# First attention: what keys to the left add, put into the strips ahead of their way through DRAM

## The chip, the cores and the metric

The kernel runs on one core of a Trainium2 chip. Its engines work side by side, each through its own queue in order: TensorE (PE: matrix products and transposes, results in PSUM), VectorE (DVE), ScalarE (ACT), GpSimd (POOL) and SyncE (SP), which here only issues DMA transfers. Engines wait for each other and for transfers by semaphores. The metric is the device time of one execution in microseconds, lower being better; for the kernel before it is 2069.74 us, the median of three runs (2066.32 to 2071.68).

## The reference, cut to what matters

The program is a stack of four layers, each added to its input: an attention with relative positions, a feed-forward layer, a second attention and a mixture of experts. Only the first attention is touched. It has 8 batches of 512 tokens, 16 heads of 16 numbers:

```python
pos_k = (rel_embeddings @ Wk + bk)             # 128 positions, per head
c2p_att = einsum('bhqd,hpd->bhqp', q, pos_k)   # query by position
c2p = take_along_axis(c2p_att, clip(rel + 64, 0, 127), axis=-1)
p2c_att = einsum('bhkd,hpd->bhkp', k, pos_k)   # key by position
p2c = swapaxes(take_along_axis(p2c_att, clip(-rel + 64, 0, 127), -1), -1, -2)
scores = (q @ k.T + c2p + p2c) / scale         # scale = sqrt(48)
probs = softmax(scores); ctx = probs @ v
```

`rel` is a bucket of the distance query minus key. Distances of 127 and more, to the left or to the right, all give the first or the last position. So a score gets two terms that depend on the distance, and each is constant far away on either side.

## The kernel before, in words

The first attention (`_l0_attention`) goes through 256 steps, numbered in the order of `steps`: batch b (8), group g of four heads (4), tile i of 128 queries (4), pair p of two heads (2). Eight steps are thus one head group, and i runs from 0 to 3 in it, two steps each.

*Strips.* For each step `strips(u)` multiplies 128 queries by 256 position columns, and 128 keys by 256 columns, for two heads (eight matmuls, L364). Column c of a strip belongs to one distance (127 - c for queries, c - 127 for keys), up to column 254. Distances beyond are the same on each side; the kernel measures the near values from the end values, so that far keys add nothing here, and folds the end values into the products of query and key through spare rows. What is then missing is a constant for keys on the left within the query's own block of 128 keys (and the like on the key side). That constant comes out of the same matmul as column 255 of the strip.

Two ACT copies bring a strip from PSUM to SBUF (L371). SP writes it to one of four DRAM buffers (`shift`, L381, 255 columns of 512). Reading it back with rows of 511 instead of 512 shifts each row by its number: distances turn into places, and the near blocks come out as query by key. Two reads do that (L390): `winp` holds the key side, which still has to be transposed, and `winc` the query side.

*The own block.* POOL multiplies column 255 by a mask of the keys on the left (`own`, L374; the masks are `later` and `earlier`, triangles of 128 by 128 in `aside`). When the reads have landed, `add()` puts `own` on the middle block of `winp` and on the block i of `winc` (two POOL adds of 128x256, L401).

*A step.* The products of query and key go into PSUM (L421). `near_keys` transposes blocks of `winp` on top of them (L433): its own block, the left and the right neighbour's. The right neighbour of step n is step n+2, which has the next i; for i = 3 there is none. DVE adds `winc` and takes the row minimum of the negated scores (L447), ACT makes the exponentials (L450), TensorE turns them (L461), DVE copies them (L464) and TensorE multiplies them by the values (L473).

*Order.* The order on every engine is written by hand (`tc.manual_schedule`). In step n come the first product, `strips(n + 5)`, then `near_keys(n)`, the rest of the products' work and what `plan` holds for that step (projections of the next group, L174; the output and layer norm of an earlier batch, L509 to L523, with POOL adds). Inside `strips(u)` the order of the issues is: own(u) on POOL, the write of u on SP, the two reads of u-1 on SP, the adds of u-2 on POOL. The reads of u-1 therefore stand behind the write of u in SP's queue.

*Buffers.* Strips have three SBUF buffers, own three, winp eight, winc eight; DRAM buffers are four.

Of the kernel before, what the change touches and what calls it, by code (L numbers as in the profile page):

```python
# [12 lines left out]
F32 = mybir.dt.float32  # L13
# [3 lines left out]
ALU = mybir.AluOpType  # L17
# [4 lines left out]
P = 128  # L22
# [6 lines left out]
W = 256  # L29
# [61 lines left out]
def _l0_attention(nc, tc, a, x, ident, mhalf, carry, prefetch):  # L91
# [6 lines left out]
    with ExitStack() as ctx:  # L98
# [20 lines left out]
        def load(b):  # L119
            nc.sync.dma_start(x[b], a["x"][b].rearrange("(t p) c -> p t c", p=P))  # L120
# [7 lines left out]
        def busy(n, w):  # L128

            idle = misc("idle")  # L130
            for _ in range(n):
                nc.tensor.matmul(idle, w[:, :P], w[:, :S], start=True, stop=True)
# [57 lines left out]
        with tc.tile_pool(name="a_pos", bufs=1) as pp:  # L190
# [14 lines left out]
            nc.sync.dma_start(rows["bv"], a["bv"].partition_broadcast(P))  # L205

            aside = wp.tile([P, 2, P], F32, tag="aside", name="aside")
            nc.sync.dma_start(aside[:, 0, :], a["later"])
            nc.sync.dma_start(aside[:, 1, :], a["earlier"])
            zeros = pp.tile([P, 8 * W], F32, tag="zeros", name="zeros")  # L210
            nc.gpsimd.memset(zeros, 0.0)
            for d in shift:
# [116 lines left out]
        sb = pool("a_sb", 2)  # L329
# [4 lines left out]
        def near(i):  # L334

            lo, hi = max(0, i - 1), min(NT, i + 2)
            return lo, hi, (lo - i + 1) * P, (hi - i + 1) * P
# [1 line left out]

        steps = [(b, g, i, p) for b in range(B) for g in range(NG) for i in range(NT) for p in range(2)]  # L340
        wins, totals = {}, {}
        reads, adds = [], []
        cns = {b: [] for b in range(B)}
        rest = []
        def project(b, g):
# [6 lines left out]
        def heads(p):  # L352

            return [slice(32 * r, 32 * r + 32) for r in (2 * p, 2 * p + 1)]

        def strips(u, between=None):


            b, g, i, p = steps[u]
            s = sm[b, g]  # L360
            pas = [ps_a.tile([P, S], F32, tag="psa", name="pa") for j in range(2)]
            for t, (src, pos) in enumerate(((s[0], posc), (s[2], posp))):
                for pa, rs in zip(pas, heads(p)):
                    nc.tensor.matmul(  # L364
                        pa[:, t * W : (t + 1) * W], src[rs, i * P : (i + 1) * P], pos[rs, g, :], start=True, stop=True
                    )
                if t == 0 and between is not None:
                    between()
            st = sb.tile([P, 4, W], F32, tag="strip", name="strip", bufs=3)
            for j in range(2):  # L370
                nc.scalar.copy(st[:, 2 * j : 2 * j + 2, :].rearrange("p t w -> p (t w)"), pas[j])  # L371

            own = sb.tile([P, 2, 2, P], F32, tag="own", name="own", bufs=3)
            nc.gpsimd.tensor_tensor(  # L374
                own,
                aside.unsqueeze(2).to_broadcast([P, 2, 2, P]),
                st[:, :, W - 1 : W].rearrange("p (j t) o -> p t j o", t=2).to_broadcast([P, 2, 2, P]),
                ALU.mult,
            )
            d = shift[u % NSHIFT]  # L380
            nc.sync.dma_start(  # L381
                bass.AP(d.tensor, d.offset + P + 1, [[2 * W, P], [2 * W * P, 4], [1, W - 1]]), st[:, :, : W - 1]
            )
            wc = winc[u % (2 * NT)]
            wk_ = sb.tile([P, 2, WIN], F32, tag="winp", name="winp", bufs=8)

            def read():
                lo, hi, c0, c1 = near(i)
                for t, dst in ((1, wk_[:, :, c0:c1]), (0, wc[:, :, lo * P : hi * P])):
                    nc.sync.dma_start(  # L390
                        dst,
                        bass.AP(
                            d.tensor,
                            d.offset + t * 2 * W * P + P + c0,
                            [[2 * W - 1, P], [4 * W * P, 2], [1, c1 - c0]],
                        ),
                    )

            def add():
                for t, dst in ((1, wk_[:, :, P : 2 * P]), (0, wc[:, :, i * P : (i + 1) * P])):  # L400
                    nc.gpsimd.tensor_tensor(dst, dst, own[:, t], ALU.add)  # L401


            reads.append(read)
            adds.append(add)
            if len(reads) > 1:
                reads.pop(0)()
            if len(adds) > 2:
                adds.pop(0)()
            wins[u] = wc, wk_  # L410

        def products(n):
# [142 lines left out]
        with tc.manual_schedule():  # L555
            for f in first:
                f(1)
            for u in range(AHEAD):
                strips(u)
                if u >= 2:  # L560
                    load(3 + u)
                if u < AHEAD - 1:
                    busy(1, posc[:, 0:2].rearrange("p g w -> p (g w)"))
            es, ets = None, deque()
            for now in range(len(steps) + 3):
                n = now
                if n < len(steps):
                    b, g, i, p = steps[n]
                    if (i, p) == (0, 0):
                        if g % 2 == 0:  # L570
                            totals[b, g // 2] = sb.tile([P, NT, 8], F32, tag="totals", name="totals", bufs=2)
                    scs, parts = products(n)
                    parts.pop(0)()
                    more = parts.pop() if parts else None
                    if n + AHEAD < len(steps):
                        strips(n + AHEAD, more)
                    else:
                        if more is not None:
                            more()
                        for todo in (reads, adds):  # L580
                            if todo:
                                todo.pop(0)()
                    new = []
                    for j in range(2):
                        near_keys(n, j, scs[j])
                        new.append(weights(n, j, scs[j]))
                if n <= len(steps):
                    if es:
                        ets.extend(turned(es))
                    es = new  # L590
                if n % 2 and len(ets) >= 4:
                    four = [ets.popleft() for _ in range(4)]
                    weigh(n - 3, four, 0)
                elif n % 2 == 0 and n >= 4:
                    weigh(n - 4, four, 1)
                for f in plan.pop(n, ()):
                    f()
                for f in prefetch.get(n - len(steps), ()):
                    f(misc, sb)
            for n in sorted(plan):  # L600
                for f in plan[n]:
                    f()
# [1075 lines left out]
def _buckets(r):  # L1678

    d = np.abs(r)  # L1680
    d = np.where(d < 32, 31, d)
    far = np.ceil(np.log(d / 32) / np.log(127 / 32) * 31 - 1e-6) + 32
    return np.where(d <= 32, d, far * np.sign(r)).astype(np.int64)


def _constants():
    onehot = np.zeros((2, P, W), np.float32)
    j = np.arange(W - 1)
    for t, r in enumerate((127 - j, j - 127)):
        place = 64 - _buckets(-r) if t else 64 + _buckets(r)  # L1690
        onehot[t, np.clip(place, 0, 127), j] += 1.0
        onehot[t, np.where(r > 0, 127, 0), j] -= 1.0
    m = np.arange(P)
    tail = np.zeros((P, 2), np.float32)
    for e, t, value in ((HD, 0, 1.0), (HD + 1, 0, -1.0), (HD + 2, 1, -SCALE), (HD + 3, 1, SCALE)):
        tail[m % 32 == e, t] = value
    i = np.arange(4)
    heads = np.zeros((P, NK, 32), np.float32)
    for k in range(NK):
        heads[m, k, NH // NK * k + m // HD] = 1.0  # L1700

    tiles = np.arange(NB).reshape(B // 2, 2, 2, 2).transpose(2, 0, 1, 3).reshape(NB)
    before = (i[None, :] < i[:, None]).astype(np.float32).reshape(16)
    return {
        "onehot": onehot,
        "tail": tail,
        "later": np.tril(np.ones((P, P), np.float32), -1),
        "before": before,
        "heads": heads,
        "pages": (P * (m[:, None] + P * np.arange(2))).astype(np.float32),  # L1710
        "earlier": np.triu(np.ones((P, P), np.float32), 1),
        "dest": (
            (P * tiles[None, :, None] + m[:, None, None]) * TOPK + np.arange(TOPK)
        ).astype(np.int32),
        "spare": (NTOK * TOPK + P * np.arange(NS)[None, :] + m[:, None]).astype(np.int32),
    }
# [20 lines left out]
def _layout(v):  # L1737
# [26 lines left out]
        "supT": v["L1_ffn_shared_up_w"].T,  # L1764
        "sdownT": v["L1_ffn_shared_down_w"].T,
        **_constants(),
    }

# [16 lines left out]
```

## Time and profile before

| what | value |
|---|---|
| median of three runs | 2069.74 us |
| the profiled execution | 2061.48 us |
| its span, first to last instruction | 2059.7 us |
| TensorE busy | 1937.6 us (94%) |
| DVE busy | 1392.4 us (68%) |
| ACT busy | 1106.3 us (54%) |
| POOL busy | 1134.0 us (55%) |
| DMA traffic | 444.46 MB, mean 216 GB/s |
| write of a strip, issue to landing | 510 KB, 4.3 us (median) |
| read of winp, issue to landing | 384 KB 4.9 us, 256 KB 4.3 us |
| read of winc, issue to landing | 384 KB 6.3 us, 256 KB 4.4 us |

In the profile a group of instructions is named by its line, engine, operation and tiles (written tile, arrow, read tiles), followed by its count, its busy time, the mean of one in ns, and how long the engine stood idle just before such an instruction and what ended most of that. PEld is TensorE's loading of weights, SPq the issuing of a DMA by SP. The first attention takes the span up to about 1070 us.

### The profile page before, as it was taken

To read this page: it belongs to the slowest core of one execution; us is meant where nothing else is said; L and a number is where in the kernel's file an instruction comes from. 1 tells how busy PE (TensorE), PEld (TensorE's weight loads), DVE (VectorE), ACT (ScalarE), POOL (GpSimd) and SP (SyncE) were. 2 spreads that over 40 slices of the span, in tenths; PEclk is the share of its full clock that TensorE was granted. 3 is DMA by queue.
4 is the path that set the end of the run, shared out by engine and by line. 5 is a ranking of instruction groups with operands and counts; after the bars stand their busy time and mean duration, and the time that the engine had idled before them with its cause. 6 is when DMAs were issued, how large, how long until landed. Compare 5 with 4: busy or idle time off the path is not lost. (4 is left out here: it accounts for less than half of the span.)

```text
span 2059.7 us, 49676 instructions
## 1 busy us (share of the span) xinstructions
PE 1937.6 (94%) x18040; PEld 1327.0 (64%) x18040; DVE 1392.4 (68%) x3727; ACT 1106.3 (54%) x2368; POOL 1134.0 (55%) x1334
## 2 busy tenths in 40 slices
PE   7999999999999999999989999999989877899997
PEld 4666666676666766766656666655555444588886
DVE  4677777677777777766776555247876786456666
ACT  3776777767777777776742211344444333144443
POOL 4666777867778677776744111014434443455555
PEclk9999999999999999999999999999999997999999
DMA  9999999999999999999974446801111114557888
GB/s 296 317 317 281 296 300 295 300 285 307 295 298 303 289 310 303 294 298 289 294 224 141 124 127 195 25 0 37 43 38 45 48 45 190 208 164 219 258 262 272
DMA packets 387522, 444.46 MB, mean 216 GB/s; under 512 B 43472, under 2 KB 368080, under 8 KB 386768
## 3 DMA queue, kind: packets, MB, share of 16 engines
q1 hardware_dynamic: 372496, 401.94, 64.3%
q0 software_dynamic: 13824, 38.29, 5.1%
q8 instruction: 146, 2.39, 0.5%
q10 hardware_dynamic: 960, 1.05, 0.2%
q14 instruction: 96, 0.79, 0.1%
HBM read 238.99 MB, written 202.19 MB: 214 GB/s over the span
## 5 line engine op out<-in xcount | busy, mean ns | idle before, releaser
L447 DVE CUSTOM_DVE_ANT_0 e<-sc,winc 128x512 f32<-128x512 f32 x512 | 333.3, 689 | 289.9 <-PE sc L433 174.1
L450 ACT ACTIVATE e<-e,low 128x512 f32<-128x512 f32 x512 | 365.6, 715 | 101.8 <-DVE low L447 100.3
L371 ACT COPY strip<-pa 128x512 f32<-128x512 f32 x512 | 275.2, 591 | 129.1 <-POOL winc L401 53.1
L374 POOL TENSOR_TENSOR own<-aside,strip 128x512 f32<-128x512 f32 x256 | 268.8, 1050 | 113.4 <-ACT strip L371 97.6
L464 DVE COPY et<-et_ps 128x512 f32<-128x512 f32 x512 | 328.5, 683 | 0.7 <-PE et_ps L461 0.7
L421 PE MATMUL sc<-sm,sm 32*128 32x256 f32 (+3 forms) x1792 | 310.0, 436 | 0.7 <-DVE low L447 0.4
L364 PE MATMUL pa<-pos,sm 32*128 32x256 f32 x2048 | 292.1, 401 | 0.1
L941 POOL DMA_INDIRECT rows<-pay,slot x128 | 141.1, 1103 | 220.3 <-issue 207.1
L401 POOL TENSOR_TENSOR winp<-winp,own 128x256 f32<-128x256 f32 x256 | 187.2, 731 | 106.3 <-DMA winp<-shift 83.7
L433 PE MATMUL sc<-ident,winp 128*128 128x128 f32 x1280 | 203.7, 287 | 30.0 <-DMA winp<-shift 29.5
L421 PEld LDWEIGHTS sc<-sm,sm 32*128 32x128 f32 x1792 | 164.3, 185 | 96.8 <-DVE et L464 35.2
L401 POOL TENSOR_TENSOR winc<-winc,own 128x256 f32<-128x256 f32 x256 | 187.1, 731 | 68.3 <-DMA winc<-shift 61.4
L941 POOL DMA_INDIRECT results<-y,r x160 | 156.3, 977 | 119.6 <-ACT y L1560 77.4
L433 PEld LDWEIGHTS sc<-ident,winp 128*128 128x128 f32 x1280 | 137.6, 142 | 108.1 <-issue 57.2
L461 PE MATMUL et_ps<-ident,e 64*128 64x64 f32 x4096 | 184.2, 230 | 1.1 <-DVE et L464 1.1
L364 PEld LDWEIGHTS pa<-pos,sm 32*128 32x128 f32 x2048 | 176.1, 185 | 10.8 <-ACT strip L371 3.9
L58 POOL TENSOR_TENSOR rstd<-var,mhalf 128x2 f32<-128x2 f32 (+1 forms) x56 | 51.0, 911 | 233.8 <-DVE var L56 210.1
L461 PEld LDWEIGHTS et_ps<-ident,e 64*128 64x128 f32 x4096 | 148.8, 140 | 44.1 <-issue 22.1
L473 PE MATMUL ctx_ps<-et,v 128*32 128x128 f32 x4096 | 168.2, 283 | 0.5 <-DVE et L464 0.5
L1540 PE MATMUL pge<-store,rT 128*128 x640 | 166.1, 382 | 1.8 <-DMA r<-rows 0.8
L174 PE MATMUL pq<-xnT,wqk 128*128 128x512 f32 x256 | 132.8, 643 | 0.7 <-PE pv L156 0.7
L738 ACT ACTIVATE hT<-ph,b 128x512 f32<-128x512 f32 x64 | 44.0, 687 | 165.6 <-PE ph L735 165.6
(222 smaller groups left out, 3340.0 us busy)
## 6 DMA issues: line engine op xcount, KB each, us to landing
shift<-strip SPq DMA_DIRECT2D x256, 510.0 KB, 4.3
winp<-shift SPq DMA_DIRECT2D x128, 384.0 KB, 4.9
winc<-shift SPq DMA_DIRECT2D x128, 384.0 KB, 6.3
winp<-shift SPq DMA_DIRECT2D x128, 256.0 KB, 4.3
winc<-shift SPq DMA_DIRECT2D x128, 256.0 KB, 4.4
rows<-empty SPq DMA_DIRECT2D x8, 2640.0 KB, 13.6
r<-rows SPq DMA_DIRECT2D x160, 132.0 KB, 2.7
z<-results SPq DMA_DIRECT2D x32, 512.0 KB, 5.6
```

The source lines that it names most:

```text
L364: nc.tensor.matmul(pa[:, t * W : (t + 1) * W], src[rs, i * P : (i + 1) * P], pos[rs, g, :], start=True, stop=True)
L371: nc.scalar.copy(st[:, 2 * j : 2 * j + 2, :].rearrange("p t w -> p (t w)"), pas[j])
L374: nc.gpsimd.tensor_tensor(own, aside.unsqueeze(2).to_broadcast([P, 2, 2, P]), st[:, :, W - 1 : W].rearrange("p (j t) o -> p t j o", t=2).t ...
L401: nc.gpsimd.tensor_tensor(dst, dst, own[:, t], ALU.add)
L421: nc.tensor.matmul(sc[:, c0:c1], s[side_][rs, cut : cut + P], s[2 + side_][rs, c0:c1], start=c0 == 0, stop=False, skip_group_check=True,)
L433: nc.tensor.matmul(sc[:, m * P : (m + 1) * P], wins[n + 2 * (m - i)][1][:, j, (i - m + 1) * P : (i - m + 2) * P], ident, start=False, stop ...
L447: nc.vector.tensor_tensor_reduce(e, sc, wins[n][0][:, j, :], 1.0, -LOW, ALU.add, ALU.min, low)
L450: nc.scalar.activation(e, e, AF.Exp, bias=low, scale=-1.0, accum_out=totals[b, g // 2][:, i, r : r + 1])
L461: nc.tensor.transpose(bank[:, c : c + 64], e[rs, m * P : (m + 1) * P], ident[rs, rs])
L464: nc.vector.tensor_copy(et[:, f].rearrange("p j m q -> p (j m q)"), bank)
L473: nc.tensor.matmul(ctx_ps[32 * r : 32 * r + 32, i * P : (i + 1) * P], vs[b % 2][:, m, g % 2, g // 2 * 4 + r, :], et[:, :, m, :], start=m = ...
L941: ins = nc.gpsimd.indirect_dma_start(to, bass.IndirectOffsetOnAxis(ap=index, axis=0), source, None, bounds_check=last)
```

## The change

The constant is added to the strip in SBUF, before it is written to DRAM, instead of to `winp` and `winc` after they were read. In a strip the own block isn't a block: row m of a strip has its left keys of the own block where m + c is at least 127 and c is under 127 (query side), or, on the key side, where the column past 128 and m sum to under 127. One array `aside` with these two masks takes the place of the two triangles. `own` is laid out as the strip is (head, side), and one POOL add of 128x512 elements puts it on the first half of the query side's columns and on the second half of the key side's, for both heads. The list `adds` and its function go.

```diff
             aside = wp.tile([P, 2, P], F32, tag="aside", name="aside")
-            nc.sync.dma_start(aside[:, 0, :], a["later"])
-            nc.sync.dma_start(aside[:, 1, :], a["earlier"])
+            nc.sync.dma_start(aside, a["aside"])
...
-            own = sb.tile([P, 2, 2, P], F32, tag="own", name="own", bufs=3)
+            own = sb.tile([P, 2, 2, P], F32, tag="own", name="own", bufs=2)
             nc.gpsimd.tensor_tensor(
                 own,
-                aside.unsqueeze(2).to_broadcast([P, 2, 2, P]),
-                st[:, :, W - 1 : W].rearrange("p (j t) o -> p t j o", t=2).to_broadcast([P, 2, 2, P]),
+                aside.unsqueeze(1).to_broadcast([P, 2, 2, P]),
+                st[:, :, W - 1 : W].rearrange("p (j t) o -> p j t o", t=2).to_broadcast([P, 2, 2, P]),
                 ALU.mult,
             )
+            nearer = st.rearrange("p (j t) (h r) -> p j (t h) r", t=2, h=2)[:, :, 0:4:3, :]
+            nc.gpsimd.tensor_tensor(nearer, nearer, own, ALU.add)
             d = shift[u % NSHIFT]
             nc.sync.dma_start(
                 bass.AP(d.tensor, d.offset + P + 1, [[2 * W, P], [2 * W * P, 4], [1, W - 1]]), st[:, :, : W - 1]
...
-            def add():
-                for t, dst in ((1, wk_[:, :, P : 2 * P]), (0, wc[:, :, i * P : (i + 1) * P])):
-                    nc.gpsimd.tensor_tensor(dst, dst, own[:, t], ALU.add)
             reads.append(read)
-            adds.append(add)
             if len(reads) > 1:
                 reads.pop(0)()
-            if len(adds) > 2:
-                adds.pop(0)()
...
-                        for todo in (reads, adds):
-                            if todo:
-                                todo.pop(0)()
+                        if reads:
+                            reads.pop(0)()
...
-        "later": np.tril(np.ones((P, P), np.float32), -1),
+        "aside": np.stack([(m + m[:, None] >= 127) * (m < 127), m + m[:, None] < 127], 1).astype(np.float32),
```

More of the change, by code (lines that the diff above doesn't have):

```diff
@@ L341, in _l0_attention @@
         wins, totals = {}, {}
-        reads, adds = [], []
+        reads = []
         cns = {b: [] for b in range(B)}
```

## The prediction

> **What bounds the kernel now.** I read the page's 40 slices first. The change touches the first attention alone, which is the first half of the span, and there TensorE is full while the DMA engines look full too. These are the rows of TensorE, of its granted clock and of the DMA engines, a digit being a tenth of full:
>
> ```profile
> PE 7999999999999999999989999999989877899997
> ...
> PEclk9999999999999999999999999999999997999999
> DMA  9999999999999999999974446801111114557888
> ```
>
> Two full rows can't both be the bound, so I asked for busy time by stretch. From 60 to 1060 us, the steady part of the first attention, TensorE works 975.5 of 1000 us:
>
> ```profile
> 60.00:1060.00 1000.00, 975.50 (x13580) 678.01 (x13582) 727.31 (x1823) 725.59 (x1640) 723.83 (x907) 0.99 0.95 298
> ```
>
> The columns are PE, PEld, DVE, ACT, POOL, then clock, DMA share, GB/s. TensorE sets the pace; the other engines have a quarter of their time free. The waits of TensorE in that stretch say what takes the rest:
>
> ```profile
> PE sc L433 <- DMA winp<-shift: 23.9, 18, 4.5
> PE sc L433 <- POOL winp L401: 0.4, 1, 0.4
> ```
>
> Nearly all its idle time is the near-key transposes (L433) waiting for a strip to come back from DRAM (total us, times, longest). So TensorE is just ahead of a long chain: strip matmuls (L364), two ACT copies (L371), a DMA write to DRAM (L381), a DMA read back (L390), then L433 of a later step. The timeline shows one strip (number 114) go through it:
>
> ```profile
> 486.52 1.07 ACT L371 COPY strip<-pa 128x512 f32<-128x512 f32 x2 [0.33 <-issue]
> ...
> 487.62 0.36 SPq L381 DMA_DIRECT2D shift<-strip  x1
> 487.74 1.05 POOL L374 TENSOR_TENSOR own<-aside,strip 128x512 f32<-128x512 f32 x1
> ...
> 492.89 0.36 SPq L390 DMA_DIRECT2D winp<-shift  x1
> ...
> 495.84 0.33 PE L433 MATMUL sc<-ident,winp 128*128 128x128 f32 x1
> ...
> 497.19 0.55 PE L433 MATMUL sc<-ident,winp 128*128 128x128 f32 x3 [1.02 <-DMA winp<-shift]
> ```
>
> The copy ends at 487.59 and the write goes out at once; POOL's own (L374) runs beside the write and delays nothing. The read is issued 5.3 us later, and TensorE, having done one transpose of step 112, stands 1.02 us until it lands.
>
> How much room there is follows from the code: strip u is made in step u-5, and step u-2 already needs its winp (right neighbour), except where i is 3. That is three steps. From the starts and landings in the trace (steps 16 to 247, means): matmuls' end to copies' end 1.18 us, issue 0.05, write 4.65, wait for the read's issue 0.36, read 4.65: 10.9 us, against three steps of 3.99 = 12.0. Subtracting each landing from the moment TensorE needs it gives a mean room of 1.4 us over 174 such steps; 151 have under 2.5 us, 24 have none. By place: at i=0, first pair, 0.4; at i=2, first pair, 1.26; others 1.2 to 2.3.
>
> **The change part by part.** On POOL it removes two adds of 128x256 per strip and puts in one of 128x512. The rows (busy us, mean ns, idle before):
>
> ```profile
> L374 POOL TENSOR_TENSOR own<-aside,strip 128x512 f32<-128x512 f32 x256 | 268.8, 1050 | 113.4 <-ACT strip L371 97.6 <-DMA x<-in_x 7.3
> L401 POOL TENSOR_TENSOR winp<-winp,own 128x256 f32<-128x256 f32 x256 | 187.2, 731 | 106.3 <-DMA winp<-shift 83.7 <-PE sc L433 8.4 <-PE pa L364 8.0
> L401 POOL TENSOR_TENSOR winc<-winc,own 128x256 f32<-128x256 f32 x256 | 187.1, 731 | 68.3 <-DMA winc<-shift 61.4 <-DVE low L447 4.1 <-ACT e L450 1.4
> ...
> L1120 POOL TENSOR_TENSOR x<-x,bproj 128x512 f32<-128x512 f32 x16 | 19.9, 1271 | 0.2
> ```
>
> The new add isn't in this trace. Nearest is L1120, two full operands of that size: 1.27 us. Bounds: 1.05 (L374, one operand a broadcast) and 1.46 (two L401). I take 1.27. POOL saves 256 x (1.46 - 1.27) = 49 us of work, worth nothing: it is 72% busy. Its waits for reads go; who waited for its adds were TensorE (4.6 us) and DVE (8): I credit 4 us.
>
> *The added wait.* The write now waits for own and the add, so per strip: 0.14 (copy to own's start, in the timeline 487.59 to 487.74) + 1.05 + 1.27 + about 0.06 to issue = 2.5 us later. The amount of DMA is the same. Behind the write on SP stands the read of the strip before it, so that goes later by the same 2.5 us; for that read TensorE waits. Nothing is taken off the path in exchange: the removed adds stood behind the read, but step u-2 uses blocks of winp that they don't touch, and the own block has some 8 us of room.
>
> *What of 2.5 us reaches TensorE.* A stall lets the strips already on their way catch up; strips made after it are late again. Those are needed from three steps on. Of eight steps (one head group), the two at i=3 need no new strip. So a group has two stalls: at i=0 (room 0.4, so 2.1 us) and, three or four steps later, at i=2 (room 1.26, so about 1.3; it covers what i=1 lacks). 32 groups x 3.4 = 109 us. Low end: if phases even out, only the loop of eight bounds. The read of strip u is issued behind the write of u+1, so from those matmuls 1.2 + 2.5 + 0.45 + 4.65 = 8.8 us must fit two steps; three such links and two free steps of 3.3 make 33.0 us against 8 x 3.99 = 31.9 now: 1.1 x 32 = 36 us. High end: 2.5 twice per group, 160.
>
> *POOL's queue.* In seven batches the layer norm's adds (L521 to L523, six of 0.73 us in each of two steps) stand before own. Today own is late by 2.6 us there (strip copied at 632.66, own at 635.22) and hurts nobody; now the write is late too. About 4 us a batch: +27 (0 to 60).
>
> *Clock.* Around a 1.9 us wait at 623 us the granted clock (the third number from the end) falls:
>
> ```profile
> 623.00:626.00 3.00, 1.14 (x18) 0.78 (x20) 0.37 (x1) 1.07 (x2) 0.72 (x1) 1.00 0.96 296
> 626.00:630.00 4.00, 4.00 (x28) 1.88 (x24) 2.79 (x8) 1.52 (x4) 2.56 (x4) 0.57 1.05 362
> ```
>
> After each of five waits of 2.0 to 3.2 us in this stage the next strips came 1.2 to 1.6 us late; after three of 0.9 to 1.2 us they did not. The Trainium skill (TensorE: Matmul & The Clock Gate, "Why this matters for your kernels") asks only that gaps stay under about 3 us. By the rule, stalls of about 2 us cost nothing more; by the row, some 16 new ones over 2 us (half of the 32 at i=0) cost 1.5 each: +24 (the sum below is 104 by the rule, 128 by the row). I take the row.
>
> *Transfers.* A stalled TensorE leaves the DMA engines emptier. The skill (DMA: Bandwidth & Descriptors, "Anatomy of one DMA") fits 2.0 us plus bytes / 436 GB/s on POOL's path: 3.2 us for the 510 KB write and 2.8 for an average 320 KB read, 6.0 together. That speaks against a loss: 3.3 us shorter than 9.3 would swallow the 2.5, and the sum would be nothing or a little below. The trace's shortest are 3.4 and 3.2, the means 4.65 each. Most of this lies in the write and two reads running side by side, which stays. Groups of eight steps with a slower mean step (3.6 to 4.3 us) show no shorter writes (correlation -0.01) and hardly shorter reads (-0.17), so by the row I take 5% off: 0.47 us at each of 64 stalls, -30 (0 to -90 at 15%).
>
> *Small things.* The first step's fill: +2.5. One load for aside instead of two, and two own buffers for three (add and next own are on one engine, in order): 0.
>
> Sum: 109 + 27 + 24 - 30 - 4 + 2.5 = 128. The profiled execution took 2061.5 us (span 2059.7), so 2190; the median of the runs shown, 2069.74, lies 8 above it. With 130 I forecast **2200 us** as median.
>
> **The rivals.**
> *A: phases even out.* Stalls shrink to the loop's own bound, +36: 2106. For it: 24 steps only have no room now. Against it: projection steps (4.8 us) and plain ones (3.1 to 3.2) alternate, and room can't be carried over them.
> *B: POOL's queue and the clock bite fully.* 160 + 60 + 32 x 1.5 - 30 = 238: 2308; halfway there, about 2255, is likelier. For it: waits and dips come together in the trace. Against it: most groups show only one place with under 1 us of room.
> *C, the other side: landings shorten.* If write and read together fell from 9.3 to 6.8 us, the 2.5 would be hidden and even today's 24 us of waits partly go: 2050 to 2070. It decides from 6.8 us down; the shortest seen are 3.4 + 3.2 = 6.6, so every transfer would have to run at its best. The DMA row at 9 speaks for it only if queueing, not the three transfers' own overlap, makes them long.
> That the change doesn't do what it says is excluded: in the instruction order POOL has 512 adds fewer and 256 more, TensorE's order is unchanged, and the write waits for POOL.
>
> **How the numbers follow.** Likeliest 0.73 (own range 2150 to 2250), A 0.12, B 0.10, C 0.05. The range to 8 in 10 leaves out C, the low part of A and the high part of B: 2115 to 2260. A measurement here tells 0.3%, 6 us, from no change. C divides into faster 0.03 and same 0.02; slower 0.95.
>
> **What would show it.** TensorE's wait for winp at the near keys 130 to 170 us instead of 30, most at i=0 and i=2; the strip add at 1.2 to 1.35 us; POOL's waits for winp and winc gone; the write issued about 2.5 us after the copies; the stage ending some 130 us later, nothing different after it; the stage's DMA near 265 GB/s (298 x 1000/1130); more dips of clock. Wrong, if landings get much shorter, if the add takes much over 1.5 us, or if stalls sit once per group instead of twice.

## The result, and the profile after

The changed kernel takes 2260.2 us (median of four runs, 2250.8 to 2270.0) against 2068.7 us for the kernel before (median of four): 9.4% longer, ratio 1.0942 (95% interval 1.091 to 1.0973). The forecast was 2200 with a range of 2115 to 2260: the direction and the kind of loss were right, the size was not.

The page of the changed kernel shows the same two rows as before the change, now with room in both; TensorE and the DMA engines are idle more over the first half of the span, and the granted clock has more dips:

```profile
PE   7889888899888888898998899999989987799997
...
PEclk8989999999899899999998999999999998799999
DMA  7888877878787778788888544490111111756887
```

By stretch (PE, PEld, DVE, ACT, POOL, clock, DMA share, GB/s), TensorE now works 880.9 us of the 1000 where it worked 975.5, at a mean clock of 0.92 instead of 0.99:

```profile
60.00:1060.00 1000.00, 880.92 (x11403) 591.10 (x11404) 617.69 (x1540) 615.70 (x1387) 577.08 (x550) 0.92 0.81 250
```

The waits of TensorE itself in the first attention, from 60 us on, are one line (total us, times, longest), where before it was 23.9 us in 18 waits:

```profile
PE sc L427 <- DMA winp<-shift: 146.1, 85, 4.4
```

TensorE loads each strip as weights before it transposes it, so the waits of its weight loads (PEld) take in some more of the same. Over the whole program, before and after:

```profile
PEld sc L433 <- DMA winp<-shift: 34.6, 26, 5.7
```

```profile
PEld sc L427 <- DMA winp<-shift: 172.4, 93, 5.8
```

L427 is the near-key transpose, L433 before. The POOL groups answer to those shown before. The new add is L380, and the adds with their waits for reads are gone:

```profile
L373 POOL TENSOR_TENSOR own<-aside,strip 128x512 f32<-128x512 f32 x256 | 268.4, 1048 | 394.5 <-ACT strip L370 345.5
...
L380 POOL TENSOR_TENSOR strip<-strip,own 128x512 f32<-128x512 f32 x256 | 325.1, 1270 | 20.1
```

One strip on its way, from the timeline of the changed kernel:

```profile
507.42 1.07 ACT L370 COPY strip<-pa 128x512 f32<-128x512 f32 x2 [0.36 <-issue]
...
508.57 1.05 POOL L373 TENSOR_TENSOR own<-aside,strip 128x512 f32<-128x512 f32 x1 [0.64 <-ACT strip L370]
...
509.69 1.26 POOL L380 TENSOR_TENSOR strip<-strip,own 128x512 f32<-128x512 f32 x1
...
510.53 0.55 PE L427 MATMUL sc<-ident,winp 128*128 128x128 f32 x3 [2.96 <-DMA winp<-shift]
510.98 0.36 SPq L382 DMA_DIRECT2D shift<-strip  x1
...
512.70 3.09 PE L174 MATMUL pq<-xnT,wqk 128*128 128x512 f32 x4
...
518.60 1.98 PE L174 MATMUL pq<-xnT,wqk 128*128 128x512 f32 x4
...
520.56 0.36 SPq L382 DMA_DIRECT2D shift<-strip  x1
521.01 0.46 SPq L391 DMA_DIRECT2D winp<-shift  x1
```

Three things are to be seen. The copies end at 508.49 and the write goes out at 510.98, 2.5 us later, with own and the add between. TensorE stands 2.96 us for an earlier strip's read. And the four projection matmuls after that stall take 3.09 us, four of the same shape in the next step 1.98: the trace has the granted clock at half from 511.5 to 514.9 us. The last two lines show a lag that feeds itself. The read at 521.01 is of the strip written at 510.98, which landed at 517.75. It waited 3.3 us more in SP's queue, behind the write of the next strip, whose matmuls the stall had made late. Over strips 16 to 247 the mean time from a write's landing to its read's issue rose from 0.36 to 1.15 us; for the strip made in the step of the stall at i=0, first pair, from 0.57 to 3.55. That strip is needed at i=1, second pair.

Where the time lies: the last near-key transpose ends at 1263.4 us instead of 1069.0, so 194 us of the profiled difference of 204 arise in the first attention. What follows took 1000.0 us instead of 990.7; in the runs below it is 995 to 1011 us whatever they change in the first attention, so I don't put this down to the change.

### The profile page after: what moved, and what is told of

Read it like the earlier page. It is cut to its first block, busy times and chain, and to the rows that moved or that the text cites. A ratio compares the mean times of both kernels' runs of the same rounds, so it can differ in the third digit from the quotient of the medians.

```text
span 2263.4 us, 48858 instructions
## 1 busy us (share of the span) xinstructions
PE 2017.2 (89%) x18040; PEld 1357.5 (60%) x18040; DVE 1395.9 (62%) x3727; ACT 1105.0 (49%) x2368; POOL 1099.3 (49%) x1078
## 3 DMA queue, kind: packets, MB, share of 16 engines
q10 hardware_dynamic: 960, 1.05, 0.1%
## 5 line engine op out<-in xcount | busy, mean ns | idle before, releaser
L427 PE MATMUL sc<-ident,winp 128*128 128x128 f32 x1280 | 225.2, 297 | 151.8 <-DMA winp<-shift 151.5
L380 POOL TENSOR_TENSOR strip<-strip,own 128x512 f32<-128x512 f32 x256 | 325.1, 1270 | 20.1
L415 PE MATMUL sc<-sm,sm 32*128 32x256 f32 (+3 forms) x1792 | 303.7, 443 | 0.1
L363 PE MATMUL pa<-pos,sm 32*128 32x256 f32 x2048 | 298.0, 408 | 0.8 <-ACT strip L370 0.7
L427 PEld LDWEIGHTS sc<-ident,winp 128*128 128x128 f32 x1280 | 140.7, 145 | 245.7 <-DMA winp<-shift 172.4
L415 PEld LDWEIGHTS sc<-sm,sm 32*128 32x128 f32 x1792 | 156.4, 189 | 104.0 <-issue 50.2
L455 PE MATMUL et_ps<-ident,e 64*128 64x64 f32 x4096 | 195.3, 240 | 1.0 <-DVE et L458 1.0
L363 PEld LDWEIGHTS pa<-pos,sm 32*128 32x128 f32 x2048 | 180.4, 189 | 12.0 <-ACT strip L370 4.6
L455 PEld LDWEIGHTS et_ps<-ident,e 64*128 64x128 f32 x4096 | 158.5, 148 | 47.4 <-issue 31.9
L467 PE MATMUL ctx_ps<-et,v 128*32 128x128 f32 x4096 | 181.5, 300 | 0.5 <-DVE et L458 0.5
L174 PE MATMUL pq<-xnT,wqk 128*128 128x512 f32 x256 | 155.1, 737 | 0.0
L185 ACT ACTIVATE sm<-pq,bias 128x512 f32<-128x512 f32 x128 | 81.0, 684 | 114.2 <-PE pq L174 107.2
```

What stands on the lines that cost most here:

```text
L363: nc.tensor.matmul(pa[:, t * W : (t + 1) * W], src[rs, i * P : (i + 1) * P], pos[rs, g, :], start=True, stop=True)
L380: nc.gpsimd.tensor_tensor(nearer, nearer, own, ALU.add)
L415: nc.tensor.matmul(sc[:, c0:c1], s[side_][rs, cut : cut + P], s[2 + side_][rs, c0:c1], start=c0 == 0, stop=False, skip_group_check=True,)
L427: nc.tensor.matmul(sc[:, m * P : (m + 1) * P], wins[n + 2 * (m - i)][1][:, j, (i - m + 1) * P : (i - m + 2) * P], ident, start=False, stop ...
L455: nc.tensor.transpose(bank[:, c : c + 64], e[rs, m * P : (m + 1) * P], ident[rs, rs])
```

## The experiments

The theory on trial (the chain): the loss is the delay of the write and of the read behind it, as far as TensorE's room doesn't cover it. Its rivals are a cost of the new instructions whatever the room, and the clock as the main part. Ratios are to the kernel before, run beside each. An end of the first attention is the end of the last near-key transpose in that run's profile (1069.0 before, 1263.4 changed).

**The delay in doses.** First with no POOL work ahead of the write:

```diff
-            own = sb.tile([P, 2, 2, P], F32, tag="own", name="own", bufs=2)
-            nc.gpsimd.tensor_tensor(own, ..., ALU.mult)
-            nearer = st.rearrange(...)[:, :, 0:4:3, :]
-            nc.gpsimd.tensor_tensor(nearer, nearer, own, ALU.add)
```

> The changed kernel with both POOL instructions of a strip (own and the add) left out, so the constant for keys on the left is missing from the scores; the write waits for the ACT copies alone, as before the change. Chain theory (the loss is the 2.5 us by which each write and the read behind it are late, as far as the room of three steps doesn't cover it): all of the loss goes, 2050 to 2075 us, TensorE's wait for winp at the near keys back to 30 us. Rival (something else in the change, such as the way strips lie in SBUF or the buffers): stays above 2150.

Measured: ratio 1.0007 (0.9991 to 1.0024), end of the first attention 1062.1 us.

With the add alone:

```diff
-            nc.gpsimd.tensor_tensor(own, ..., ALU.mult)
...
-            nc.gpsimd.tensor_tensor(nearer, nearer, own, ALU.add)
+            nc.gpsimd.tensor_tensor(nearer, nearer, aside.unsqueeze(1).to_broadcast([P, 2, 2, P]), ALU.add)
```

> The changed kernel with the product own left out: the add puts the bare mask on the strip, one POOL instruction of 128x512 ahead of the write, which is late by about 1.4 us instead of 2.5. Chain theory, with the landings of the trace before carried forward step by step: about 95 us over before, 2165 (2140 to 2190). Rival (only the sum of POOL's work or the add's own traffic in SBUF counts): near the full change, above 2220, since the add is still there. Even-phases rival (no loss until the loop of eight is full): under 2110.

Measured: ratio 1.0482 (1.0447 to 1.0517), end 1174.0 us.

With the add twice:

```diff
             nc.gpsimd.tensor_tensor(nearer, nearer, own, ALU.add)
+            nc.gpsimd.tensor_tensor(nearer, nearer, own, ALU.add)
```

> The changed kernel with the add made twice (the constant is counted double), so that the write is late by about 3.8 us. Chain theory, carried forward: about 260 us over before, 2330 (2290 to 2370), TensorE's wait for winp about 245 us. If the loss is not by the delay but a fixed cost of the new order: 2260 to 2275.

Measured: ratio 1.1437 (1.14 to 1.1474), end 1370.1 us; 2379 us, above what was expected. TensorE's waits for winp in the first attention, in the order none, add alone, add twice:

```profile
PE sc L418 <- DMA winp<-shift: 27.6, 28, 4.1
```

```profile
PE sc L420 <- DMA winp<-shift: 97.6, 60, 4.4
```

```profile
PE sc L428 <- DMA winp<-shift: 215.8, 90, 5.5
```

So with a write late by 0.03, 1.44, 2.50 (the change) and 3.87 us (medians), the loss is 0, 100, 195 and 297 us of 2069 (from the ratios). That is some 71 to 79 us for each us, nearly a straight line through nothing. It tells the delay from the rest of the change: the one load of the masks and the order of the issues are in the first of these runs and cost nothing (own and its two buffers are not in it; they come back in the run with seven steps below). And no threshold of covered delay shows: at 1.44 us already there is a loss of 100. Smaller delays were not tried.

**More room instead of less delay.** Strips made six steps ahead:

```diff
-AHEAD = 5
+AHEAD = 6
...
-            wk_ = sb.tile([P, 2, WIN], F32, tag="winp", name="winp", bufs=8)
+            wk_ = sb.tile([P, 2, WIN], F32, tag="winp", name="winp", bufs=9)
...
-                slot((n + 8 * g - 8, n + 8 * g - 7), project(b, g))
+                early = 1 if b or g > 1 else 0
+                slot((n + 8 * g - 8 - early, n + 8 * g - 7 - early), project(b, g))
```

> The changed kernel with strips made six steps ahead instead of five (nine winp buffers for eight, the projections one step earlier); all is computed. Chain theory: one step of 3.1 to 4.8 us more room against 2.5 us of delay: most of the loss goes, 2060 to 2110, wait for winp under 50 us. Rival (the add itself or the clock is what costs, whatever the room): above 2200.

Measured: ratio 1.0861 (1.0828 to 1.0895), 2259 us. By the time alone the rival had won. The profile says otherwise: the wait is gone, and TensorE is full, 1169.6 of the 1180 us from 60 to 1240 (columns as above).

```profile
L427 PE MATMUL sc<-ident,winp 128*128 128x128 f32 x1280 | 198.8, 286 | 6.2 <-DMA winp<-shift 6.2
```

```profile
60.00:1240.00 1180.00, 1169.56 (x13544) 811.45 (x13546) 743.58 (x1826) 734.07 (x1641) 685.91 (x653) 0.99 0.83 253
```

The timeline of this run shows what TensorE is full of. Products (L415) and strip matmuls (L363) follow one another:

```profile
561.62 0.72 PE L415 MATMUL sc<-sm,sm 32*128 32x256 f32 x4
562.16 0.61 PE L363 MATMUL pa<-pos,sm 32*128 32x256 f32 x4
562.59 0.61 PE L415 MATMUL sc<-sm,sm 32*128 32x256 f32 x4
563.02 0.61 PE L363 MATMUL pa<-pos,sm 32*128 32x256 f32 x4
```

In the kernel before they ran at once (products L421, strips L364):

```profile
505.81 0.60 PE L421 MATMUL sc<-sm,sm 32*128 32x128 f32 x4
505.93 0.60 PE L364 MATMUL pa<-pos,sm 32*128 32x256 f32 x4
```

A step's products use the 64 rows of one pair of heads, and its strips those of the pair of step n + AHEAD. With an odd number these are the other rows, with an even one the same. The experiment had changed two things. With seven (ten winp buffers, three et buffers, the projections one step earlier):

```diff
-AHEAD = 5
+AHEAD = 7
...
-            wk_ = sb.tile([P, 2, WIN], F32, tag="winp", name="winp", bufs=8)
+            wk_ = sb.tile([P, 2, WIN], F32, tag="winp", name="winp", bufs=10)
...
-            et = sb.tile([P, 2, 2, NT, 64], F32, tag="et", name="et", bufs=4)
+            et = sb.tile([P, 2, 2, NT, 64], F32, tag="et", name="et", bufs=3)
...
-                slot((n + 8 * g - 8, n + 8 * g - 7), project(b, g))
+                start = n + 8 * g - 9
+                slot((max(start, 0), start + 1), project(b, g))
```

> The changed kernel with strips made seven steps ahead (ten winp buffers, three et buffers for four, projections one step earlier); all is computed. With six, TensorE's wait for winp fell from 151.5 to 6.2 us, yet the time stayed at 2259: the strip matmuls then used the same rows of TensorE as the products beside them (the same pair of heads), and the two no longer ran at once. Seven makes the pairs differ again. Chain theory: no wait for winp worth naming and no serial matmuls: at or a little below the kernel before, 2020 to 2075. Rival (the POOL instructions ahead of the write cost by themselves): above 2200 again.

Measured: ratio 1.0049 (1.0032 to 1.0066), 2091 us, a little above what was expected, with the same POOL work ahead of the same writes. The first near-key transpose starts at 54.4 us instead of 43.6 (seven strips go ahead of it instead of five), and the first attention ends at 1080.5, 11.5 later than before the change: of the 194 us, 11 are left as the longer start and less than 1 as the rest. The waits, of TensorE at the near keys:

```profile
L427 PE MATMUL sc<-ident,winp 128*128 128x128 f32 x1280 | 198.1, 286 | 2.4 <-DMA winp<-shift 2.4
```

Six and seven together show that parity made the 2259: with seven, the wait is as good as gone and the matmuls overlap. The wait's end did not bring a gain over the kernel before: between the first and the last near-key transpose TensorE is idle for 14 us instead of 31, but busy for 1012 instead of 995. What makes these some 17 us was not settled.

The same seven steps in the kernel before, with own in two buffers and its adds one place earlier in POOL's queue, was to beat both:

```diff
-AHEAD = 5
+AHEAD = 7
...
+            if len(adds) > 1:
+                adds.pop(0)()
-            own = sb.tile([P, 2, 2, P], F32, tag="own", name="own", bufs=3)
+            own = sb.tile([P, 2, 2, P], F32, tag="own", name="own", bufs=2)
```

> The kernel before (adds after the reads) with strips made seven steps ahead, own in two buffers, et in three, projections one step earlier; all is computed. Chain theory: its 30 us of wait for winp and most of the falls of clock after them go: 2020 to 2055, so faster than both kernels. If those waits were only taking the place of others: 2065 to 2075.

Measured: ratio 1.012 (1.0087 to 1.0153), slower than the kernel before. The waits for winp are gone from TensorE (0.0 us at L433), but the start is 8 us longer, and a wait that wasn't there stands in the list of waits:

```profile
PE spread L497 <- POOL wide L489: 25.3, 14, 3.7
```

POOL's adds wait for reads in front of wide, which TensorE needs for its quotients. This wait took the place of those for winp: from the first to the last near-key transpose TensorE is idle for 37 us where it was 31. It is also busy for 1011 us instead of 995, as in the changed kernel with seven. With the start these are the 31 us by which the first attention ends later (8, 6 and 17). Whether the adds' new place in the queue makes the wait for wide was not tried apart.

**The clock.** Four matmuls without use ahead of the near keys of each group's first step, where the longest stalls stand:

```diff
+FILL = 4
...
+                    if (i, p) == (0, 0) and n:
+                        busy(FILL, posc[:, 0:2].rearrange("p g w -> p (g w)"))
                     new = []
                     for j in range(2):
                         near_keys(n, j, scs[j])
```

> The changed kernel with four matmuls without use (128x512, about 2.6 us together) ahead of the near keys of the first step of each head group, where the longest waits stand. Clock theory (a part of the loss is the halved clock after each wait, not the waiting): the waits are filled at no cost, the clock stays up, 20 to 60 us less than the changed kernel: 2200 to 2240, granted clock from 0.94 to over 0.955. If the clock is not worth naming: the fillers' excess over the waits comes on top, 2260 to 2300.

Measured: ratio 1.0836 (1.08 to 1.0872) against 1.0942, 2255 us, between the two expectations; mean clock 0.966 instead of 0.94. The first attention ends 25 us earlier, at 1238.3, of which 5 are an earlier start. TensorE's idle time from the first to the last near-key transpose fell by 73 us, and the useless matmuls took 80 (31 x 4 x 0.64), so by these two alone the stage would have been 7 us longer; it was 20 shorter. The time at half clock, from 60 us on, falls from 177.5 to 64.8 us. A part of the loss is the clock.

**POOL's queue.** Without the norm's scale and bias:

```diff
-                    nc.gpsimd.tensor_tensor(xn[:, t, :], xn[:, t, :], rows["ln_scale"], ALU.mult)
-                    nc.gpsimd.tensor_tensor(xn[:, t, :], xn[:, t, :], rows["ln_bias"], ALU.add)
```

> The changed kernel without the scaling and the bias of the first layer's norm: eight of the twelve POOL instructions of 0.73 us that stand in POOL's queue ahead of own in two steps of each batch (the values of the layer are thus others). Queue theory (about 27 us of the loss come from writes that are late behind these): 15 to 25 us less than the changed kernel, 2235 to 2245. If the queue doesn't reach TensorE: within 5 us of it.

Measured: ratio 1.0785 (1.075 to 1.082), 2247 us, just above the range of the queue theory, the first attention ending at 1243.7, 20 us earlier. Of these, 5 us are an earlier start; without it 15 are left, and the weight loads' waits for winp fell by 11. These eight of twelve instructions stand for 18 of the 27 us, so the size of the term is about right.

**The place of the stalls.** Only the projections one step earlier, in the kernel before and in the changed one:

```diff
-                slot((n + 8 * g - 8, n + 8 * g - 7), project(b, g))
+                start = n + 8 * g - 9
+                slot((max(start, 0), start + 1), project(b, g))
...
-            slot((n + 24, n + 25), project(b + 1, 0))
+            slot((n + 23, n + 24), project(b + 1, 0))
```

> The kernel before with each head group's two projections one step earlier, so that one of them (1.3 us of TensorE) stands in the last step of the group ahead, in front of the near keys of i=0, first pair, where 30 of its 35 us of waits for winp lie; all is computed. Room theory: 1.3 us more room there; 15 to 25 us of waits and some falls of clock go: ratio to the kernel before 0.980 to 0.993. If these waits only stand in for others: within 0.3%.

Measured: ratio 1.0055 (1.0038 to 1.0073): a miss. The waits at i=0, first pair, did fall, from 30 to 11 us (weight loads, here and in the next run), but TensorE's time from the last near-key transpose of a step to the next step's strips grew by 20 us over the stage, and the waits at i=1 and i=2 from 4 to 15. What makes those 20 us was not settled.

> The same in the changed kernel, all computed. Room theory: 31 of 32 groups have 1.3 us more room at their first stall (some 90 of its 172 us of waits), so 20 to 50 us less than the changed kernel: ratio to the kernel before 1.070 to 1.085 where the change had 1.094. If the stalls are set by the loop of eight steps alone, in which the same work only changes its place: 1.090 to 1.098.

Measured: ratio 1.0819 (1.0762 to 1.0875), as expected in size; but by place the waits fell at i=0, first pair, from 87 to 45 us and rose at i=1, second pair, from 28 to 75. Room given at one place is mostly taken back at the next.

## Why the prediction was wrong

**Right: what bounds, and the mechanism.** TensorE ahead of the chain, the added wait of 2.5 us (2.50 measured as median), nothing taken off the path, and SP's queue behind it. The doses and the seven steps ahead show this, and rule out that the add as such costs anything worth naming. The new add took 1.27 us as taken.

**Right, in part by luck: the stalls.** They were put at 109 us with two per group, and 27 for POOL's queue, together 136. The weight loads' waits for winp rise from 35 to 172 us: 138. By place: +57 at i=0, first pair (67 was meant), +28 at i=1, second pair, +47 at i=2, first pair, +6 elsewhere. The place of the second stall was foreseen at i=2 alone. The sum counted the read as late by the 2.5 us of the write and put the further lag in SP's queue at nothing; it came to 0.8 us more in the mean, and to 3.0 for the strip needed at i=1, second pair. So a total that leaves this out and still meets the waits was in part lucky. The low end, in which phases even out, was not reached at any dose.

**Wrong: "Transfers".** This step took off 30 us, since landings would shorten by 0.47 us at each stall. They hardly did. A write lands after 4.42 us (mean) instead of 4.65, a read after 4.73 instead of 4.65: 0.15 us for both, while the DMA engines moved 250 GB/s instead of 298. By the step's own reckoning this is 10 us (0.15 x 64). The trace before had shown that landings do not follow the pace of the steps; I took the 5% against that row. What they go with in both traces is the number of the chain's other transfers in flight: a write took 3.95 us with fewer than 2.5 of them, and 5.74 before and 5.46 after with 3 or more. That number fell only from 2.7 to 2.4. The estimate of 6.0 us for write and read together, worked out from what the Trainium skill (DMA: Bandwidth & Descriptors, "Anatomy of one DMA") gives for POOL's path, isn't met either: they took 9.15.

**Wrong: "Clock".** The price was about right, the count not. Windows at half clock in the first attention, from 60 us on, rose from 7 to 40, so 33 new ones where I had 16, since I counted stalls at i=0 alone. (The 7 lasted 3.4 us each; of the 40, 12 lasted twice as long.) TensorE's time from the last near-key transpose of a step to the end of the next step's strips rose from 796 to 840 us over the stage, 45 us for 33 windows, 1.35 each where 1.5 was taken: 45 instead of 24. So the clock is about a quarter of the loss, not its main part. The fillers show from the other side that it is a cause. By the Trainium skill's rule (gaps under about 3 us are safe) only 13 waits of TensorE at the near keys, against 3 before, would have cost anything; 37 were of 2 us and more, and 35 of these were followed by a window at half clock.

Together: the waits were put at 102 us (109 + 27 - 30 - 4) and are 138. Of the 36 us between, 20 are the landings, 4 the credit for POOL's waits, which was not seen, and 12 stand against the lag in SP's queue; that they are this lag isn't shown. The clock was 21 too little. The start was later by 6 us where 2.5 were taken (3.5), but in the runs with fillers, with the short norm and with early projections it was later by 1 to 2 us only, so most of it belongs to this one profile. 128 + 36 + 21 + 3.5 = 189 of the 194 us; the other 6 lie within the near-key transposes beyond their waits, and their cause stays open. Rival B (the queue and the clock in full) was named with about 2255 as its likelier point and a chance of 0.10; the result is 5 us above that point and just past the range. Two slips of 1 us in the sums don't bear on this: seven batches of 4 us are 28, not 27, and 1.1 x 32 is 35, not 36.

## What to carry to other kernels

A wait put in front of a transfer costs by the room of whoever waits at the far end, and that room has to be taken step by step from a trace, by place, not from a mean: an engine that is "only" 55% busy was here worth 75 us for each us of its latency. A read that is queued behind the next write inherits the stall that made that write late, so a stall can feed the next one. Don't count on transfers getting faster because the kernel got slower (here 0.15 of 9.3 us), and count a half-clock window for each stall of over 2 us. When a lead or a buffer count is changed to test this, see what else depends on it: one step more of lead switched off the overlap of two sets of matmuls, and the time alone would have told the wrong story.

## What the runs showed of the hardware

- Clock. Over the twelve traces here, of waits of TensorE at the near keys of 0.3 to 1.5 us, 2 of 215 saw a window at half clock begin in the wait or within 3.5 us of its end; of those of 1.5 to 2 us, 36 of 67; of those of 2 us and more, 185 of 203. The Trainium skill (TensorE: Matmul & The Clock Gate, "Why this matters for your kernels") asks for gaps under about 3 us; here 2 us were enough, and the measurement decides. In the timeline above four matmuls of one shape took 3.09 us with the clock at half and 1.98 in the next step.
- Matmuls of 32 rows run at once on different rows and one after the other on the same: in the lines above, four and four of them took 0.72 us overlapped and 1.15 us in turn (the products there were 128 and 256 columns wide). The same section says that such matmuls run concurrently when they land in distinct row groups; that an even lead takes this away is what the run with six steps adds.
- Landings. Write and read of a strip followed how many of the chain's other transfers were in flight (correlation 0.76 for writes and 0.53 for reads before, 0.64 and 0.41 after).
- POOL: 1.05 us for a 128x512 product in which one operand is a broadcast column, 1.27 for the add of two full operands, also in place and over strided halves.
